# Four graph layers on one core: the weights' transfers issued by ScalarE instead of SyncE

## The chip, the cores and the metric

The kernel runs on one core of one Trainium2 chip. The time is the device time of one execution in microseconds, and several executions of the same kernel are compared by their median. A profile is one further execution, recorded instruction by instruction. The engines are named PE (TensorE), DVE (VectorE), ACT (ScalarE), POOL (GpSimd) and SP (SyncE, which here only issues transfers). Each engine takes its instructions in the order in which they were written down for it, and waits where an instruction needs another engine's result.

## The reference

64 graphs of 256 nodes with 512 features go through four layers. Each layer normalises, applies a ReLU, and adds what a graph layer makes of it to the residual `x`. Everything is float32.

```python
h = jnp.maximum(_layernorm(x), 0.0)
x = x + _L0_gnn_ref(h, adj, W_qk, W_v)                  # layer 0: masked score sums, softmax over nodes, times v
h = jnp.maximum(_layernorm(x), 0.0)
x = x + _L1_gnn_ref(h, adj, W, b, a_self, a_neigh)      # layer 1: graph attention, 8 heads of 64
h = jnp.maximum(_layernorm(x), 0.0)
x = x + _L2_gnn_ref(h, adj, Wp, bp, C)                  # layer 2: tanh(A * (Xc Xp^T)) Xp, 8 heads
h = jnp.maximum(_layernorm(x), 0.0)
x = x + _L3_gnn_ref(h, adj, nodemask, Wqk, Wv)          # layer 3: gated by q . (adj k), softmax over nodes, times v
```

## The kernel before

One graph at a time would leave every engine waiting, so the kernel overlaps about five graphs. The work of a graph is cut into some 120 named steps (`load`, `at`, `st0`, `hn0`, `sq0`, `sw0`, `ht0`, `qk0` and so on), and each step has a due time in a table. `TIMES` holds the steady state; graph `b` is due 60.2 us after graph `b-1`. The first six and the last five graphs have tables of their own (`FIRST`, `LAST`). A further table, `WEIGHTS`, gives due times to the steps that fetch and prepare the weights; these lie among the first graphs' steps. `Plan.sequence` sorts all steps of all graphs by due time, `Plan.run` writes them down in this order, and each engine's instructions are tied to that order. A due time is thus only a place in a queue; no clock is waited for.

The steps of a graph that matter here:

- `load` (L627): SP issues `x`, the adjacency rows `adj`, and the adjacency in 32x32 blocks `blocks`, four transfers by quarter.
- `st`, `rs`, `pw`, `sh`, `hn` (L652 to L681): layer norm and ReLU. DVE takes the statistics, POOL the power, DVE the shift, ACT writes `hn` (L680).
- `sq`, `sw`, `ht` (L685 to L696): the transposition of `hn`. DVE transposes 32x32 squares into `sq` (L613), SP sends `sq` to DRAM as `sq_d` (L700), and SP gathers `ht` from it in four transfers (L618). `ht` is what PE multiplies with the weights.
- `qk0`, `qk1`, `qe0`, `qe1` (L748 to L761): the query and key products of layer 0, and ACT's copies of them out of PSUM (L758). `score0` (L763) needs both copies; the value products `pv01` and `pv00` (L703, with `wv0_s`) stand behind it in PE's order.
- `fa0`, `fa1` (L789): the products of layer 1, with `w1_s`.
- `ea`, `ex` (L891, L914): ACT's Prelu and Exp of the attention.

The steps of the weights: `wqk`, `wv0`, `wv3` (L484, four transfers each), `w10` to `w13` and `w20` to `w23` (L490, four transfers each), `b1` and `b2` (L498), `c2` (L512, two), `wa` (L519, two), `mk` (L537), and `wn0` to `wn3` (L555, two each, one for each part of the product of layer 3's query and key weights). `mt`, `mv` and `mm` compute that product on PE and DVE, `sa` folds layer 1's attention vectors into its weights on DVE, and `ma` scales the product into `m3_s` on ACT.

Where a buffer is used several times, `take` and `done` (L400, L407) hand it from step to step through a first-in first-out list.

Of the kernel before, what the change touches and what calls it, by code (L numbers as in the profile page):

```python
# [16 lines left out]
P = 128  # L17
D = 512
KC = D // P
N = 256  # L20
NC = N // P
H = 8
# [365 lines left out]
class Graph:  # L388
# [5 lines left out]
    def step(self, name):  # L394
        def add(run):
            self.steps[name] = run
            return run
        return add
# [19 lines left out]
def tile_four_gnn_layers(ctx: ExitStack, tc: tile.TileContext, x, adj, nodemask,  # L418
# [5 lines left out]
    nc = tc.nc  # L424
# [14 lines left out]
    def keep(kind, count, shape, pool=None):  # L439

        plan.pools[kind] = [(pool or held).tile(shape, F32, name=f"{kind}{i}") for i in range(count)]
# [29 lines left out]
    c2_s = consts.tile([P, HP, P], F32)  # L471
# [5 lines left out]
    def weights():  # L477

        g = Graph(plan)
        step = g.step  # L480
        st = {}


        def plain(name, t, src):  # L484
            @step(name)
            def _():
                for r in range(4):
                    nc.sync.dma_start(t[r::4], src.rearrange("(k r d) e -> r d k e", k=KC, r=4)[r])

        def by_heads(name, k, t, src):  # L490
            @step(f"{name}{k}")
            def _():
                for r in range(4):
                    first = k * P + r * S
                    nc.sync.dma_start(t[r::4].rearrange("p (h u) -> p h u", h=H),
                                        src[:, first:first + S, :].rearrange("h d u -> d h u"))

        def to_all(name, t, src):  # L498
            @step(name)
            def _():  # L500
                nc.sync.dma_start(t, src.rearrange("h u -> (h u)").partition_broadcast(P))
        plain("wqk", wqk0_s, wqk0)
        plain("wv0", wv0_s, wv0)
        plain("wv3", wv3_s, wv3)
        for k in range(KC):
            by_heads("w1", k, w1_s[:, k, E:], w1)
            by_heads("w2", k, w2_s[:, k], w2)
        to_all("b1", b1_bc, b1)
        to_all("b2", b2_bc, b2)


        @step("c2")  # L512
        def _():
            for s in range(2):
                half = slice(s * U, (s + 1) * U)
                nc.sync.dma_start(c2_s[half, :, half], c2t.rearrange("(a s) k j -> s k a j", s=2)[s])


        @step("wa")  # L519
        def _():  # L520
            st["a"] = once.tile([P, 2, D], F32, name="a_bc", bufs=1)
            for s, a in enumerate((a_self, a_neigh)):
                nc.sync.dma_start(st["a"][:, s], a.rearrange("h u -> (h u)").partition_broadcast(P))

        def times_a(k):
            @step(f"sa{k}")
            def _():
                for s in range(2):
                    prod = once.tile([P, D], F32, name="prod", bufs=1)
                    nc.vector.tensor_mul(prod, w1_s[:, k, E:], st["a"][:, s])  # L530
                    nc.vector.tensor_reduce(w1_s[:, k, s * H:(s + 1) * H], prod.rearrange("p (h u) -> p h u", h=H),
                                            AX.X, OP.add)
        for k in range(KC):
            times_a(k)


        @step("mk")  # L537
        def _():
            st["mask"] = once.tile([B, N], F32, name="mask_rows", bufs=1)
            nc.sync.dma_start(st["mask"], nodemask)  # L540

        @step("mkp")
        def _():
            pm = g.take("bank", name="mask")
            for c in range(NC):
                nc.tensor.transpose(pm[:, c * B:(c + 1) * B], st["mask"][:, c * P:(c + 1) * P], ident[:B, :B])

        @step("mkv")
        def _():
            nc.vector.tensor_copy(mask_c, g["mask"][:, :NC * B].rearrange("p (c b) -> p c b", c=NC))  # L550
            g.done("mask")


        def part_of_m(e):
            @step(f"wn{e}")  # L555
            def _():
                st[f"wn{e}"] = w_n = once.tile([P, 2, KC, P], F32, name="w_n")
                for s in range(2):
                    first = s * D + e * P
                    nc.sync.dma_start(w_n[:, s], wqk3[:, first:first + P].rearrange("(k p) e -> p k e", p=P))  # L560

            @step(f"mt{e}")
            def _():
                for s in range(2):
                    pt = g.take("bank", name=f"wt{s}")
                    for k in range(KC):
                        nc.tensor.transpose(pt[:, k * P:(k + 1) * P], st[f"wn{e}"][:, s, k], ident)

            @step(f"mv{e}")
            def _():  # L570
                st["w_t"] = w_t = once.tile([P, 2, D], F32, name="w_t", bufs=1)
                nc.vector.tensor_copy(w_t[:, 0, :].rearrange("p (k d r) -> p k d r", k=KC, r=4),
                                      g["wt0"].rearrange("p (k r d) -> p k d r", k=KC, r=4))
                nc.vector.tensor_copy(w_t[:, 1, :], g["wt1"])
                g.done("wt0")
                g.done("wt1")

            @step(f"mm{e}")
            def _():
                for k in range(KC):  # L580
                    pm = g[f"m{k}"] if e else g.take("bank", name=f"m{k}")
                    nc.tensor.matmul(pm, st["w_t"][:, 0, k * P:(k + 1) * P], st["w_t"][:, 1, :],
                                     start=(e == 0), stop=(e == KC - 1))
        for e in range(KC):
            part_of_m(e)

        @step("ma")
        def _():
            for k in range(KC):
                nc.scalar.activation(m3_s[:, k, :], g[f"m{k}"], AF.Copy, scale=1.0 / math.sqrt(D))  # L590
                g.done(f"m{k}")


        @step("room")
        def _():
            setup.close()
            late = ctx.enter_context(tc.tile_pool(name="late", bufs=1, side="right"))
            keep("xp", 2, [P, NC, D], late)
            keep("xpt", 2, [P, HP, N], late)
            keep("xc", 1, [P, HP, N], late)  # L600
        return g
# [567 lines left out]
```

## Time and profile before

| | us |
|---|---|
| timed runs | 3900.15, 3894.99, 3899.66; median 3899.66 |
| profiled execution | 3905.45, of which 3903.3 from first to last instruction |
| PE busy | 3811.1 |
| DVE busy | 3033.7 |
| ACT busy | 1704.9 |
| POOL busy | 1264.8 |
| bytes moved | 717.62 MB, 184 GB/s in the mean |

A row of the groups reads: line, engine, operation, output and inputs, count, then the busy time in all and the mean of one in ns, then the engine's idle time just before these instructions and what ended most of it. The largest groups of PE are the products with the gathered `ht`:

```profile
L607 PE MATMUL bank<-w_s,ht 128*128 128x256 f32 (+2 forms) x3072 | 963.4, 464 | 30.6 <-DMA ht<-sq_d 24.5
L607 PE MATMUL bank<-wv_s,ht 128*128 128x512 f32 x2048 | 914.4, 594 | 0.1
```

A row of the time-ordered view reads: start, length, engine, line, operation, count, and in brackets the idle time before it and what ended it. A row with x4 is four neighbouring instructions run together. SPq marks SP's queue: the length is the time that SP spent on issuing, not the transfer. All transfers of the program are on one queue:

```profile
q1 hardware_dynamic: 1657328, 714.19, 74.7%
```

### The profile page before, as it was taken

What the parts mean: (1) busy time and instruction counts of PE and PEld (TensorE: products, weight loads), DVE (VectorE), ACT (ScalarE), POOL (GpSimd) and SP (SyncE); (2) the same over time, 40 slices, a digit from 0 to 9 for tenths busy, and PEclk for the clock granted to TensorE, in tenths of its full rate; (3) what the DMA queues carried; (4) which work ended last, traced back from release to release, by engine and by line L of the source; (5) the groups of instructions that cost most, each with busy time, mean ns of one, the idle gap of its engine ahead of it and who ended that gap; (6) DMA issues with size and microseconds to landing.
All of it is one profiled execution on the core that took longest, in us unless ns stands there. A gap on an engine that the chain in (4) does not pass through costs nothing.

```text
span 3903.3 us, 53632 instructions
## 1 busy us (share of the span) xinstructions
PE 3811.1 (98%) x17474; PEld 2375.3 (61%) x17474; DVE 3033.7 (78%) x7641; ACT 1704.9 (44%) x3333; POOL 1264.8 (32%) x1098
## 2 busy tenths in 40 slices
PE   7999999999999999999999999999999999999989
PEld 4756566566566666666666666666566665665564
DVE  6887778777877877877777788788788778777774
ACT  2444444444444444444444444444444444444342
POOL 1332323323323323323323333333233233233231
PEclk9999999999999999999999999999999999999989
DMA  8666777777777788777777877777778777777754
GB/s 211 174 189 172 179 194 174 196 193 179 194 189 184 194 185 189 192 185 181 190 186 186 196 182 187 191 181 191 191 176 200 187 181 192 187 179 193 172 145 107
DMA packets 1657607, 717.62 MB, mean 184 GB/s; under 512 B 1493936, under 2 KB 1549296, under 8 KB 1632752
## 3 DMA queue, kind: packets, MB, share of 16 engines
q1 hardware_dynamic: 1657328, 714.19, 74.7%
q8 instruction: 140, 2.29, 0.3%
q14 instruction: 139, 1.14, 0.1%
HBM read 477.56 MB, written 236.45 MB: 183 GB/s over the span
## 4 chain that ended last, share of the span: by engine, by line
PE 74%; DVE 7%; DMA 4%; SPq 2%; issue 1%; POOL 1%; ACT 1%; DVEq 0%; POOLq 0%; ACTq 0%
PE bank L607 44%; PE bank L928 10%; PE bank L1016 6%; PE bank L1030 5%; PE bank L1102 5%; PE bank L994 3%; DVE junk L852 2%; DVE sq L613 1%; DMA hn<-sq_d 1%; SPq L618 1%; DMA ht<-sq_d 1%; DVE shift L673 1%; PE bank L768 1%; PE bank L718 1%; DVE stats L657 1%
## 5 line engine op out<-in xcount | busy, mean ns | idle before, releaser
L607 PE MATMUL bank<-w_s,ht 128*128 128x256 f32 (+2 forms) x3072 | 963.4, 464 | 30.6 <-DMA ht<-sq_d 24.5
L607 PE MATMUL bank<-wv_s,ht 128*128 128x512 f32 x2048 | 914.4, 594 | 0.1
L607 PEld LDWEIGHTS bank<-w_s,ht 128*128 128x128 f32 x3072 | 572.9, 192 | 364.4 <-issue 215.6
L607 PEld LDWEIGHTS bank<-wv_s,ht 128*128 128x128 f32 x2048 | 380.8, 191 | 426.2 <-issue 410.8
L904 POOL TENSOR_TENSOR pair<-pair,negt 128x1024 f32<-128x1024 f32 x256 | 600.5, 2367 | 50.6 <-ACT pair L897 46.4
L680 ACT ACTIVATE hn<-xt,shift,rstd 128x512 f32<-128x512 f32 x512 | 388.7, 806 | 448.6 <-DVE shift L673 430.3
L928 PEld LDWEIGHTS bank<-feats,pair 128*128 128x128 f32 x4096 | 485.0, 194 | 47.9 <-issue 25.5
L897 ACT ACTIVATE pair<-all,ec 128x256 f32<-128x256 f32 x1024 | 417.2, 494 | 200.1 <-DMA all<-er_d 196.3
L928 PE MATMUL bank<-feats,pair 128*128 128x65 f32 x4096 | 480.8, 276 | 10.2 <-ACT pair L916 10.2
L1055 ACT ACTIVATE pair<-pair 128x512 f32<-128x512 f32 x512 | 294.8, 623 | 420.6 <-DVE pair L1048 420.2
L852 DVE CUSTOM_DVE_ANT_0 junk<-all,adj 128x256 f32<-128x256 f32 x1024 | 444.0, 434 | 35.2 <-DMA all<-er_d 2.1
L607 PE MATMUL bank<-m_s,ht 128*128 128x512 f32 x1024 | 465.9, 599 | 1.3 <-DVE pair L1048 0.8
L668 POOL TENSOR_TENSOR rstd<-rstd,power 128x2 f32<-128x2 f32 x256 | 180.6, 706 | 813.4 <-DVE rstd L664 804.9
L1048 DVE TENSOR_TENSOR pair<-bank,at 128x512 f32<-128x512 f32 x512 | 327.4, 683 | 107.7 <-PE bank L1016 107.0
L1083 POOL TENSOR_TENSOR xt<-xt,hn 128x512 f32<-128x512 f32 x64 | 111.5, 1742 | 924.6 <-DMA hn<-sq_d 657.9
L613 DVE STREAM_TRANSPOSE sq<-hn 128x512 f32<-128x512 f32 x512 | 337.7, 690 | 58.9 <-ACT hn L680 58.9
L657 DVE BATCH_NORM_STATS2 stats<-xt 128x6 f32<-128x512 f32 x512 | 327.2, 680 | 36.4 <-POOL xt L1083 28.6
L910 DVE TENSOR_TENSOR pair<-pair,all 128x1024 f32<-128x1024 f32 x256 | 325.9, 1292 | 9.9 <-DMA all<-m_d 7.5
L607 PEld LDWEIGHTS bank<-m_s,ht 128*128 128x128 f32 x1024 | 189.2, 190 | 213.5 <-issue 207.1
L953 POOL TENSOR_TENSOR xt<-xt,o 128x256 f32<-128x256 f32 x256 | 181.2, 729 | 386.6 <-DVE rs L941 225.1
L916 ACT ACTIVATE pair<-pair 128x1024 f32<-128x1024 f32 x256 | 262.2, 1047 | 45.1 <-DVE pair L910 39.6
L1016 PE MATMUL bank<-xc,xpt 64*128 64x256 f32 x2048 | 255.8, 389 | 1.8 <-ACT xc L1002 1.0
(77 smaller groups left out, 3866.9 us busy)
## 6 DMA issues: line engine op xcount, KB each, us to landing
sq_d<-sq SPq DMA_DIRECT2D x384, 512.0 KB
ht<-sq_d SPq DMA_DIRECT2D x1024, 128.0 KB
all<-er_d SPq DMA_DIRECT2D x128, 1024.0 KB
all<-m_d SPq DMA_DIRECT2D x64, 1024.0 KB
xt<-in_x_dram SPq DMA_DIRECT2D x64, 512.0 KB
xpt<-sq_d SPq DMA_DIRECT2D x256, 128.0 KB
hn<-sq_d SPq DMA_DIRECT2D x256, 128.0 KB
out_dram<-xt SPq DMA_DIRECT2D x64, 512.0 KB
```

Source lines behind the costliest of these rows:

```text
L607: nc.tensor.matmul(p, ht[:, k, c * P:(c + 1) * P], w[:, k], start=(k == 0), stop=(k == KC - 1))
L613: nc.vector.transpose(sq.rearrange("p (r k c i) -> p c k r i", r=4, k=KC, c=NC)[:, c], t[:, c])
L657: nc.vector.bn_stats(stats[:, c, :], g["xt"][:, c, :])
L680: nc.scalar.activation(hn[:, c, :], g["xt"][:, c, :], AF.Relu, bias=st["shift"][:, c:c + 1], scale=st["rstd"][:, c:c + 1])
L852: nc.vector.tensor_tensor_reduce(junk, g["en"][:, h, :], g["adj"][:, c, :], 1.0, -BIG, OP.add, OP.max, st["mx"][:, c, h:h + 1])
L897: nc.scalar.activation(e[:, s, j, :], g["es"][:, h, :], AF.Prelu, bias=st["ec"][:, j, H + h:H + h + 1], alpha=0.2)
L904: nc.gpsimd.tensor_tensor(e, e, g["negt"][:, None].to_broadcast([P, 2, NC, N]), OP.add)
L910: nc.vector.tensor_tensor(e, e, g["m"][:, 2 * p:2 * p + 2, None, :].to_broadcast([P, 2, NC, N]), OP.subtract)
L928: nc.tensor.matmul(po[:, h % 4, :], e[:, s, j, i * P:(i + 1) * P], feats[:, j, h, :], start=(j == 0), stop=(j == NC - 1))
L1016: nc.tensor.matmul(ps[s][:, m, :], g["xpt"][half, p, m * P:(m + 1) * P], g["xc"][half, p, :], start=True, stop=True)
L1048: nc.vector.tensor_tensor(th[:, s], g[f"ps{p}{s}"].rearrange("p (m n) -> p m n", m=NC), g["at"], OP.mult)
L1055: nc.scalar.activation(g[f"th{p}"][:, s], g[f"th{p}"][:, s], AF.Tanh)
```

## The change

The 59 transfers that the weights' steps issue go out from ACT's queue. The steps stay where they were in the plan. The PSUM banks that `mt` takes also get the part's number in their name; the names are a key in a dictionary.

```diff
         def plain(name, t, src):
                 for r in range(4):
-                    nc.sync.dma_start(t[r::4], src.rearrange("(k r d) e -> r d k e", k=KC, r=4)[r])
+                    nc.scalar.dma_start(t[r::4], src.rearrange("(k r d) e -> r d k e", k=KC, r=4)[r])
...
         def by_heads(name, k, t, src):
-                    nc.sync.dma_start(t[r::4].rearrange("p (h u) -> p h u", h=H),
+                    nc.scalar.dma_start(t[r::4].rearrange("p (h u) -> p h u", h=H),
...
         def to_all(name, t, src):
-                nc.sync.dma_start(t, src.rearrange("h u -> (h u)").partition_broadcast(P))
+                nc.scalar.dma_start(t, src.rearrange("h u -> (h u)").partition_broadcast(P))
...
-                nc.sync.dma_start(c2_s[half, :, half], c2t.rearrange("(a s) k j -> s k a j", s=2)[s])
+                nc.scalar.dma_start(c2_s[half, :, half], c2t.rearrange("(a s) k j -> s k a j", s=2)[s])
...
-                nc.sync.dma_start(st["a"][:, s], a.rearrange("h u -> (h u)").partition_broadcast(P))
+                nc.scalar.dma_start(st["a"][:, s], a.rearrange("h u -> (h u)").partition_broadcast(P))
...
-            nc.sync.dma_start(st["mask"], nodemask)
+            nc.scalar.dma_start(st["mask"], nodemask)
...
-                    nc.sync.dma_start(w_n[:, s], wqk3[:, first:first + P].rearrange("(k p) e -> p k e", p=P))
+                    nc.scalar.dma_start(w_n[:, s], wqk3[:, first:first + P].rearrange("(k p) e -> p k e", p=P))
...
-                    pt = g.take("bank", name=f"wt{s}")
+                    pt = g.take("bank", name=f"wt{s}{e}")
...
-                g.done("wt0")
-                g.done("wt1")
+                g.done(f"wt0{e}")
+                g.done(f"wt1{e}")
```

More of the change, by code (lines that the diff above doesn't have):

```diff
@@ L572, in _ @@
                 nc.vector.tensor_copy(w_t[:, 0, :].rearrange("p (k d r) -> p k d r", k=KC, r=4),
-                                      g["wt0"].rearrange("p (k r d) -> p k d r", k=KC, r=4))
-                nc.vector.tensor_copy(w_t[:, 1, :], g["wt1"])
-                g.done("wt0")
-                g.done("wt1")
+                                      g[f"wt0{e}"].rearrange("p (k r d) -> p k d r", k=KC, r=4))
+                nc.vector.tensor_copy(w_t[:, 1, :], g[f"wt1{e}"])
+                g.done(f"wt0{e}")
+                g.done(f"wt1{e}")
             @step(f"mm{e}")
```

## The prediction

> **What bounds the kernel now.** I read the page's first two parts, then stage windows, then the time-ordered view of the first 130 us. The page:
>
> ```profile
> span 3903.3 us, 53632 instructions
> PE 3811.1 (98%) x17474; PEld 2375.3 (61%) x17474; DVE 3033.7 (78%) x7641; ACT 1704.9 (44%) x3333; POOL 1264.8 (32%) x1098
> ```
>
> TensorE (PE) is busy 3811.1 of 3903.3 us, so 92.2 us of PE idleness is all that a better order can win. Where it lies, from the stage windows (start:end, length, busy time and count per engine, PE clock, DMA share, GB/s):
>
> ```profile
> 0.00:100.00 100.00, 72.05 (x269) 43.69 (x270) 65.72 (x162) 25.36 (x52) 18.37 (x26) 0.97 0.82 210
> 100.00:200.00 100.00, 95.40 (x478) 70.85 (x478) 81.28 (x208) 44.08 (x85) 37.08 (x32) 0.91 0.71 174
> 1000.00:2000.00 1000.00, 993.98 (x4616) 622.36 (x4615) 793.81 (x2016) 450.99 (x883) 331.38 (x288) 1.00 0.77 188
> ```
>
> 28.0 us of it is in the first 100 us, 4.6 in the second; in the steady part only 0.6%. The weights' transfers all lie before 146 us. So the change can only shift the start, and PE, nearly full after 500 us, carries a shift to the end. The start (start us, length, engine, line, operation; the bracket gives the idle time before it and its releaser; SPq is SyncE's queue):
>
> ```profile
> 12.96 0.55 SPq L700 DMA_DIRECT2D sq_d<-sq  x1
> 20.11 2.65 SPq L488 DMA_DIRECT2D wv_s<-in_L_gnn_W_v_dram  x4
> 22.81 2.57 SPq L495 DMA_DIRECT2D w_s<-in_L_gnn_W_dram  x4
> 24.23 0.27 ACT L758 COPY qk<-bank 128x128 f32<-128x128 f32 x1 [5.95 <-PE bank L607]
> 25.12 0.27 ACT L758 COPY qk<-bank 128x128 f32<-128x128 f32 x1 [0.63 <-PE bank L607]
> 25.44 0.88 PE L768 MATMUL bank<-qk,at 128*128 128x64 f32 x6 [0.18 <-ACT qk L758]
> 26.44 3.67 PE L607 MATMUL bank<-wv_s,ht 128*128 128x512 f32 x8
> 34.71 2.02 PE L607 MATMUL bank<-wqk_s,ht 128*128 128x128 f32 x16 [0.94 <-DMA ht<-sq_d]
> 38.26 1.52 ACT L680 ACTIVATE hn<-xt,shift,rstd 128x512 f32<-128x512 f32 x2 [1.16 <-DVE shift L673]
> 42.48 0.38 SPq L700 DMA_DIRECT2D sq_d<-sq  x1
> 53.06 5.47 PE L607 MATMUL bank<-w_s,ht 128*128 128x272 f32 x16 [2.68 <-DMA ht<-sq_d]
> ```
>
> The weights go out from SP in time: the first Wv matmul at 26.44 waits for nothing. The two query copies of graph 0 stand 0.9 us apart on ScalarE (ACT), and PE needs the second at once.
>
> **What the Trainium skill says.** DMA: Bandwidth & Descriptors, section Issuing engines are not separate DMA queues: transfers of all issuing engines share the same DMA engines, and a second issuer saves only sequencer time; the page of before shows one busy hardware queue, so no run here bears on it yet. Perfetto Trace Analysis, section DMA Instruction — HWDGE: a recorded issue begins once its semaphores are satisfied and ends when the sequencer is free for its next instruction. The trace agrees as far as it goes: SP's issues follow each other without overlap, 602 to 968 ns each for w2. TensorE: Matmul & The Clock Gate, section What's actually happening: the PE clock halves after idling. The trace agrees: after 2.68 us of idling the w1 matmuls at 53.06 take 5.47/16 = 342 ns, the same form at 125.99 takes 5.61/24 = 234 ns.
>
> **The change, part by part.** 59 weight transfers leave SP's queue; their issue times in the time-ordered view add up to 42.4 us, 0.72 us each (8 w_n 5.55, 4 wqk 2.65, 2 a 1.40, 4 wv0 2.65, 16 w1 11.63, 2 b 1.03, 16 w2 11.43, mask 0.79, 2 c2 1.28, 4 wv3 3.94). They enter ACT's in-order queue at the same steps. ACT's other work, and all of PE, DVE and POOL, keep their order. The renamed PSUM banks (wt0 to wt00 and so on) cost nothing: the order of takes and returns, and PE's order in the built program, are unchanged. No trace has a DMA issue on ACT; I price it between SP's undisturbed 0.60 and its mean 0.72 us, taking 0.65.
>
> A second thing follows from the built program's waits. All transfers rotate over eight completion semaphores, and each issue first waits until the last user of its semaphore has landed. In the new program both queues share the eight, so an ACT issue can wait for an SP transfer, with ACT's arithmetic behind it.
>
> (1) *Graph 0 to its first ht: a gain.* sq was ready at 9.73 (the DVE transposes start at 8.31 and take 1.42) but sq_d left at 12.96, after graph 1's loads, which stood behind w_n and wqk (1.17 + 2.65 us of issue). That hold of 3.2 us goes. Against it, xt now competes with w_n from the start: 512 KB at this stretch's 210 GB/s is 2.5 us, so the delay is 0 to 2.5; I take 0.9. Net -2.3 (bounds -3.2 to -0.7).
>
> (2) *The second query copy: the large loss.* Between the two copies stand wv0 x4 and w1 x4. Without waiting: 22.2 (first copy's end, 24.5 - 2.3) + 8 x 0.65 = 27.4, against 25.12 before. With the shared semaphores the fourth wv0 waits for the last quarter of graph 1's ht: ht0's issues end at 20.07 - 2.3 = 17.8; sq_d takes 3.4 (25.48 to 28.90), four ht issues 3.3, landing 2.5 (32.17 to 34.71): 27.0. Then five issues, 3.2: 30.2. So the score and value matmuls behind the copy, and all of PE, come +2.3 to +6 later; I take +5.2, the gain of (1) already inside. The gain of graph 1's sq_d (ready at 19.03, issued at 25.48) is worthless, since PE reaches graph 1 only after this.
>
> (3) *PE clock.* PE idles about 6 us before those matmuls instead of 0.2. At the price of the 53.06 row, 16 x 108 ns = 1.7; bounds 0 to 1.7, taken 1.
>
> (4) *hn of graph 0, layer 1.* w_n x2 and w1 x4 now stand between graph 1's second query copy (ended 37.10) and hn (38.26): 6 x 0.65 = 3.9 up to the 5.5 they took on SP, less the 1.1 that ACT waited for the shift: +2.8 to +4.4. Returned: sq was complete at 40.82 while sq_d left SP at 42.48, 1.7. Net +1.1 to +2.7, taken +2, all onto PE, which was idle 2.68 us for this ht at 53.06.
>
> (5) *The rest, nearly nothing.* The fourth w1 group, w2's first three, mask, c2 and w_n fall into ACT's idle stretches (6.05 us before 51.70, 6.74 before 59.18, 7.19 before 72.78, 5.63 before 85.54, 6.93 before 94.82). wv3, at some 143 us, is hidden by 10.2 us of ACT idleness before 156.2. Only w2's last four meet a busy ACT (96.25 to 103.7): 2.6 us before the Prelu of the next graph, of which I put 0 to 2 on PE, taken 0.8.
>
> (6) *Given back.* From 100 to 500 us PE idles 18.4 us; part of it shrinks when PE is late and the others are not. 0 to 4, taken -1.
>
> Sum: 5.2 + 1 + 2 + 0.8 - 1 = **+8.0 us**, on the profiled span 3911.3. Bounds: 2.3 + 0 + 1.1 + 0 - 4 = -0.6, and 6 + 1.7 + 2.7 + 2 = +12.4. The profiled execution, 3905.45, is 5.8 above the timed median of 3899.66 (3894.99 to 3900.15); the shift added to that median gives **3908**.
>
> **Rivals.** *SP's relief wins.* ACT's issues are short and the semaphore waits are satisfied when reached. Then (1)'s -2.3 to -3.2 stays, and (2) falls away if the second copy starts before 25.1. For it: SP held sq_d three times, by 3.2, 6.4 and 1.7 us, and ACT is 25% busy in the first 100 us. Against: even without a wait, eight issues at 0.60 put the copy at 27.0. A lucky clock could help: the PE clock is 0.5 from 101 to about 117 us at full work, some 7 us that another phase may not lose. Time: 3899.7 - 3, less 0 to 7 for the clock: 3890 to 3897, about 3893.
>
> *Hidden.* Loss (2) is its no-wait size and the rest sits in the 33 us of PE idleness of the first 200: +2 to +6, about 3903. For it: small terms; against: step (4)'s ht is already what PE waits for.
>
> *Semaphores chain further.* The waits between queues pass from group to group, for example an ACT issue held by ht, holding hn, holding the next sq_d and ht. Each turn costs the 3.4 to 3.5 us of an sq_d landing; two more turns than I counted give +15, 3915.
>
> That the change does nothing is excluded: the built program has the issues on ACT.
>
> **How the numbers follow.** A measurement of this kernel can tell about 0.2%, 7.8 us, from no change. The forecast, its size around +8: 0.45, of it 0.27 above the bound and 0.18 within. Hidden: 0.22, within. Chained: 0.23, above. Relief: 0.10, below. So slower 0.27 + 0.23 = 0.50, within 0.18 + 0.22 = 0.40, faster 0.10. The range takes the forecast's bounds, half of relief below and the nearer part of chained above: 3895 to 3917; the forecast alone has 3899 to 3912.
>
> **What would show it.** After: DMA issues on ACT from 0.7 us; the first sq_d near 10.6; the second query copy of graph 0 at 27 to 31; the first Wv matmul at 28 to 32, with an idle time from ACT; hn at 45 to 47 instead of 38.26; the w1 matmuls at 60 to 62 instead of 53.06; steady windows unchanged. If the first Wv matmul comes before 27, or the w1 matmuls before 55, I am wrong in the start; if these are late and the end is not, step (6) is too small.

## The result

The changed kernel takes 3924.98 us in the median of four runs (3919.33 to 3930.32), the kernel before 3897.71 beside it (3894.99 to 3900.15). The ratio is 1.007, with a 95% interval of 1.0053 to 1.0087: +27 us, between 21 and 34. A later comparison of the same two kernels gave 1.0062 (1.0046 to 1.0077), +24 us. The forecast was +8. The direction was right, the size a third of what came.

The page of the changed kernel, its first two parts:

```profile
span 3917.5 us, 53618 instructions
PE 3811.3 (97%) x17474; PEld 2375.6 (61%) x17474; DVE 3037.3 (78%) x7641; ACT 1704.8 (44%) x3333; POOL 1262.0 (32%) x1098
```

PE has the work it had (3811.3 against 3811.1 us), and ACT too. The 14.2 us by which the span grew are idleness of PE. They are fewer than the 27 us of the medians because this profile is of the shortest of the four runs (3919.33), while that of the kernel before (3905.45) is of an execution longer than its four timed ones. The stage windows (start:end, length, busy time and count per engine, PE clock, DMA share, GB/s) say where:

```profile
0.00:100.00 100.00, 62.54 (x216) 36.51 (x216) 52.77 (x130) 19.56 (x43) 14.74 (x24) 0.90 0.77 176
100.00:200.00 100.00, 88.58 (x439) 66.16 (x440) 86.42 (x216) 43.85 (x84) 33.56 (x29) 0.91 0.69 184
1000.00:2000.00 1000.00, 994.33 (x4611) 621.31 (x4611) 792.80 (x2016) 449.24 (x882) 333.34 (x288) 1.00 0.78 187
```

PE idles 37.5 us in the first 100 (28.0 before) and 11.4 in the second (4.6 before). The steady part is as it was. The time-ordered view of the changed kernel, the rows that answer those shown of before (ACTq is ACT's queue, with the time spent on issuing and on waits between the issues of one row):

```profile
14.78 1.41 SPq L700 DMA_DIRECT2D sq_d<-sq  x1
24.78 2.05 PE L607 MATMUL bank<-wqk_s,ht 128*128 128x128 f32 x16 [0.78 <-DMA ht<-sq_d]
25.97 0.27 ACT L758 COPY qk<-bank 128x128 f32<-128x128 f32 x1 [5.19 <-PE bank L607]
25.98 7.63 ACTq L488 DMA_DIRECT2D wv_s<-in_L_gnn_W_v_dram  x4
33.65 5.43 ACTq L495 DMA_DIRECT2D w_s<-in_L_gnn_W_dram  x4
39.12 0.27 ACT L758 COPY qk<-bank 128x128 f32<-128x128 f32 x1 [12.88 <-DMA w_s<-in_L_gnn_W_dram]
39.43 1.54 PE L768 MATMUL bank<-qk,at 128*128 128x64 f32 x6 [12.44 <-ACT qk L758]
40.77 6.41 PE L607 MATMUL bank<-wv_s,ht 128*128 128x512 f32 x8
57.04 0.81 ACT L680 ACTIVATE hn<-xt,shift,rstd 128x512 f32<-128x512 f32 x1 [4.07 <-DMA w_s<-in_L_gnn_W_dram]
59.33 0.34 SPq L700 DMA_DIRECT2D sq_d<-sq  x1
69.32 5.59 PE L607 MATMUL bank<-w_s,ht 128*128 128x272 f32 x16 [2.16 <-DMA w_s<-in_L_gnn_Wp_dram]
```

Three things are to be seen. The first query products start at 24.78 instead of 23.04, although SP was to be relieved. The two query copies stand 13.1 us apart, with eight DMA issues between them, and PE waits 12.44 us for the second. The first Wv products last 6.41 us instead of 3.67. Together the first w1 products (69.32 against 53.06) are 16.3 us late. A further loss comes after this row; it is on VectorE, where the forecast had not looked. The time-ordered view of the changed kernel, VectorE, GpSimd and PE from 85 us:

```profile
85.65 0.41 DVE L852 CUSTOM_DVE_ANT_0 junk<-all,adj 128x256 f32<-128x256 f32 x1
92.97 9.26 POOL L904 TENSOR_TENSOR pair<-pair,negt 128x1024 f32<-128x1024 f32 x4 [12.04 <-ACT pair L897]
93.26 2.08 DVE L736 TENSOR_SCALAR w<-w,tot 128x2 f32<-128x2 f32 x1
95.45 2.21 DVE L865 TENSOR_SCALAR low<-mx 128x16 f32<-128x16 f32 x1
97.70 2.27 DVE L866 SCALAR_TENSOR_TENSOR low<-mx,low 128x16 f32<-128x16 f32 x1
100.00 2.26 DVE L867 TENSOR_TENSOR mx<-mx,low 128x16 f32<-128x16 f32 x1
102.98 0.38 PE L873 MATMUL bank<-ident,mx 128*8 128x128 f32 x2 [3.32 <-DVE xt L742]
```

Four operations on a few elements last over 2 us each, as long as one of GpSimd's four operations L904 beside them, and PE waits 3.32 us for what follows. The same stretch of the kernel before, from a second profile of it (b_again below):

```profile
68.32 0.42 DVE L852 CUSTOM_DVE_ANT_0 junk<-all,adj 128x256 f32<-128x256 f32 x1 [0.67 <-DMA all<-er_d]
76.48 0.17 DVE L866 SCALAR_TENSOR_TENSOR low<-mx,low 128x16 f32<-128x16 f32 x1
76.69 0.17 DVE L867 TENSOR_TENSOR mx<-mx,low 128x16 f32<-128x16 f32 x1
77.02 9.27 POOL L904 TENSOR_TENSOR pair<-pair,negt 128x1024 f32<-128x1024 f32 x4 [15.27 <-ACT pair L897]
```

Here the same operations take 0.17 us, and VectorE is done at 76.86, 0.16 us before GpSimd begins. Between the first w1 products and PE's first products with `pair` (L928) the changed kernel needs 50.0 us (69.32 to 119.35), the kernel before 45.2 in its first profile and 44.6 in its second. So 16.3 us are lost at the start and 4.8 more here: 21.1 at L928 against the first profile, 22.9 against the second, which lies within the interval of the time.

### The profile page after: what moved, and what is told of

It reads as the page before. It is cut to its first block, busy times and chain, and to the rows that moved or that the text cites. A ratio compares the mean times of both kernels' runs of the same rounds, so it can differ in the third digit from the quotient of the medians.

```text
span 3917.5 us, 53618 instructions
## 1 busy us (share of the span) xinstructions
PE 3811.3 (97%) x17474; PEld 2375.6 (61%) x17474; DVE 3037.3 (78%) x7641; ACT 1704.8 (44%) x3333; POOL 1262.0 (32%) x1098
## 4 chain that ended last, share of the span: by engine, by line
PE 73%; DVE 7%; DMA 4%; SPq 2%; issue 1%; POOL 1%; ACT 1%; DVEq 0%; POOLq 0%; ACTq 0%
PE bank L607 43%; PE bank L928 10%; PE bank L1016 6%; PE bank L1030 5%; PE bank L1102 5%; PE bank L994 3%; DVE junk L852 3%; DVE sq L613 2%; DMA hn<-sq_d 1%; SPq L618 1%; DVE shift L673 1%; DMA ht<-sq_d 1%; PE bank L768 1%; PE bank L718 1%; SPq L1076 1%
## 5 line engine op out<-in xcount | busy, mean ns | idle before, releaser
L607 PE MATMUL bank<-w_s,ht 128*128 128x256 f32 (+2 forms) x3072 | 960.9, 463 | 30.2 <-DMA ht<-sq_d 21.4
L904 POOL TENSOR_TENSOR pair<-pair,negt 128x1024 f32<-128x1024 f32 x256 | 600.4, 2366 | 53.0 <-ACT pair L897 44.8
L928 PEld LDWEIGHTS bank<-feats,pair 128*128 128x128 f32 x4096 | 485.5, 195 | 47.3 <-issue 28.1
L928 PE MATMUL bank<-feats,pair 128*128 128x65 f32 x4096 | 481.2, 276 | 9.9 <-ACT pair L916 9.9
L852 DVE CUSTOM_DVE_ANT_0 junk<-all,adj 128x256 f32<-128x256 f32 x1024 | 440.0, 430 | 34.4 <-DMA all<-er_d 1.1
```

Of the source, the lines that this page charges most:

```text
L607: nc.tensor.matmul(p, ht[:, k, c * P:(c + 1) * P], w[:, k], start=(k == 0), stop=(k == KC - 1))
L852: nc.vector.tensor_tensor_reduce(junk, g["en"][:, h, :], g["adj"][:, c, :], 1.0, -BIG, OP.add, OP.max, st["mx"][:, c, h:h + 1])
L904: nc.gpsimd.tensor_tensor(e, e, g["negt"][:, None].to_broadcast([P, 2, NC, N]), OP.add)
L928: nc.tensor.matmul(po[:, h % 4, :], e[:, s, j, i * P:(i + 1) * P], feats[:, j, h, :], start=(j == 0), stop=(j == NC - 1))
```

## Experiments

Times are ratios to the kernel before on the same chip; 0.001 is 3.9 us. "First Wv" is the start of the first Wv products on PE, "first w1" that of the first w1 products.

### The start

**e0_after_again** is the changed kernel, once more.

> The changed kernel once more, beside the others on one chip: 1.005 to 1.009 of before, if the 27 us between the medians are more than the 18 us by which PE is late at 140 us of the profile.

1.0062 (1.0046 to 1.0077). First Wv 39.15, first w1 65.86. The loss is stable, its parts vary by a few us between executions (PE idles 11.15 us here and 12.44 there).

**e1_only_wv0_w1**: the kernel before, with only the twelve transfers `wv0`, `w11` and `w10` on ACT.

```diff
-                    nc.sync.dma_start(t[r::4], src.rearrange("(k r d) e -> r d k e", k=KC, r=4)[r])
+                    (nc.scalar if name == "wv0" else nc.sync).dma_start(t[r::4], src.rearrange("(k r d) e -> r d k e", k=KC, r=4)[r])
...
-                    nc.sync.dma_start(t[r::4].rearrange("p (h u) -> p h u", h=H),
+                    (nc.scalar if f"{name}{k}" in ("w10", "w11") else nc.sync).dma_start(t[r::4].rearrange("p (h u) -> p h u", h=H),
```

> Kernel before, with only the 12 transfers of wv0, w11 and w10 on ACT, the other 47 on SP as before. Theory A (the hold of the second query copy of graph 0 behind these issues is the loss): the two copies are 8 to 13 us apart instead of 0.9, the first Wv matmul comes at 34 to 40 instead of 26.4, and the time is 1.003 to 1.007 of before, most of what the whole change costs. Theory B (the loss is spread over many groups of transfers, each with its own wait): the copies may be apart, but the time is within 1.002 of before.

1.0034 (1.0022 to 1.0046), +13 us. The first query products come at 22.86, the copies at 24.06 and 38.82, first Wv at 40.47. These twelve transfers make about half of the loss by themselves.

**e2_all_but_wv0_w1**: the reverse, the changed kernel with these twelve back on SP.

```diff
-                    nc.scalar.dma_start(t[r::4], src.rearrange("(k r d) e -> r d k e", k=KC, r=4)[r])
+                    (nc.sync if name == "wv0" else nc.scalar).dma_start(t[r::4], src.rearrange("(k r d) e -> r d k e", k=KC, r=4)[r])
...
-                    nc.scalar.dma_start(t[r::4].rearrange("p (h u) -> p h u", h=H),
+                    (nc.sync if f"{name}{k}" in ("w10", "w11") else nc.scalar).dma_start(t[r::4].rearrange("p (h u) -> p h u", h=H),
```

> Changed kernel, with wv0, w11 and w10 back on SP, the other 47 transfers on ACT. Theory A: the copies are 0.9 us apart again and the time is within 0.9985 to 1.002 of before. Theory B: the time keeps at least half of the loss, 1.0035 or more.

1.0022 (1.0013 to 1.0031), +9 us, between the two theories. The copies are 0.9 us apart, and still a third of the loss is there: +13 and +9 add up to nearly the whole. The query products start at 25.61. So the narrow account, in which everything is the second query copy, is not enough.

**e5_hold_long** and **e7_hold_short** put nothing but a hold into the kernel before: 28 and 12 idle ACT operations between the two copies of graph 0. Their results are not used.

```diff
+                if b == 0 and c == 1:
+                    hold = work.tile([P, N], F32, name="hold", tag="scratch", bufs=1)
+                    for _ in range(28):
+                        nc.scalar.activation(hold, wqk0_s[:, 0:2].rearrange("p k e -> p (k e)"), AF.Relu)
```

> Kernel before, all transfers on SP, with 28 idle activations (their result is not used) on ACT between the two query copies of graph 0, some 11 to 15 us: the hold alone, without any transfer on ACT. Theory A: PE is late by 11 to 15 us behind it, the groups of 130 us stay late by about as much, and the time is 1.003 to 1.006 of before. If a late start is made good later (theory D), the time is within 1.002.

> Kernel before with 12 idle activations on ACT between the two query copies of graph 0, 5 to 6.5 us: the size of eight issues at 0.65 us without any wait. Theory A: PE is 5 to 6 us late behind it, and the time is 1.001 to 1.002 of before, clearly less than with the long hold. So much the issues alone would cost; the rest of the change's loss is then waiting for landings.

With 28, PE idles 11.85 us ahead of the score products and the time is 1.0023 (1.0014 to 1.0032), +9 us, less than expected; with 12 it idles 4.69 us and the time is 1.001 (1.0004 to 1.0017), +4 us. A hold at this place costs about 0.8 us for each us, and keeps costing it to the end: 9.0/11.85 and 3.9/4.69 (the intervals of both include 1). By this estimate the changed kernel's 12.44 us are worth some 10 us.

**e3_copies_first**: the changed kernel with `wv0` and `w11` planned behind the second copy.

```diff
-    "wn0": 292.900, "mt0": 293.000, "wqk": 293.100, "mv0": 294.200, "wa": 294.700, "mm0": 295.100, "wv0": 295.500,
-    "w11": 295.600, "w10": 296.200, "sa1": 296.700, "sa0": 297.000, "wn1": 298.500, "w13": 298.600, "mt1": 299.000,
+    "wn0": 292.900, "mt0": 293.000, "wqk": 293.100, "mv0": 294.200, "wa": 294.700, "mm0": 295.100, "wv0": 295.910,
+    "w11": 295.920, "w10": 296.200, "sa1": 296.700, "sa0": 297.000, "wn1": 298.500, "w13": 298.600, "mt1": 299.000,
```

> Changed kernel, with the due times of wv0 and w11 put just behind the second query copy of graph 0, so that ACT makes both copies first and issues then. Theory A in the narrow sense (the copy is what matters): copies 0.9 us apart, time near before, 1.000 to 1.002. Rival C (the late arrival of Wv is what matters, and the copy was only the first to show it): PE waits for wv0 itself, issued from about 27 us and landed at some 37, so the first Wv matmul comes at 34 to 40 and the time is still 1.003 to 1.007.

1.0056 (1.0044 to 1.0068): nothing gained beyond the spread. The copies are adjacent (26.66 and 27.56), but the time-ordered view has now the wait one step on:

```profile
40.05 5.35 PE L607 MATMUL bank<-wv_s,ht 128*128 128x512 f32 x8 [11.29 <-DMA w_s<-in_L_gnn_W_dram]
```

The weights themselves come too late. (The bracket names `w_s`, since transfers share semaphores; the semaphores that these products wait for are those of the four `wv0`, of which the last was issued at 35.55.) In ACT's order a transfer goes out only after ACT's earlier arithmetic, and this arithmetic waits for PE's query products. On SP nothing of that kind stood ahead of them: `wv0` left at 20.11, before the query products had begun. Ahead of the copy they hold it, behind it they are late; both cost 11 to 12 us of PE.

**e6_wv0_early**: they are planned ahead of ACT's waits instead (`wv0` at 293.750, `w11` at 294.750, otherwise the changed kernel).

> Changed kernel, with wv0 due right behind graph 0's hn and w11 behind the attention vectors, that is issued on ACT from some 9 us, before graph 1's hn. Theory A: no issue stands between the query copies, which are 0.9 us apart; PE is at most 4 us late from the earlier traffic and graph 1's hn held behind w11; time 0.999 to 1.003. If the shared semaphores by themselves cost as much (theory E), graph 1's hn, its sq_d and ht move by 8 us or more and the time stays at 1.004 or more.

1.0037 (1.0024 to 1.005). First Wv moves from 40.77 to 32.07, and the time falls by about 10 us, to just above theory A's range. But now PE waits 3.16 us for the query products, which start at 26.62: the early weights go out beside the first graphs' loads.

**e4_pool_queue**: all 59 go out from GpSimd's queue, with eight semaphores of their own (in each of the change's lines `nc.gpsimd.dma_start`).

> All 59 weight transfers on GpSimd's queue at the same places. In the built program its transfers rotate over eight completion semaphores of their own, so SP's never wait for them nor they for SP's, and ACT holds no transfer. Theory A (in-order hold plus shared semaphores): copies of graph 0 are 0.9 us apart, SP's first sq_d leaves by 12, and the time is 0.998 to 1.002 of before. Rival (any second queue costs, since its packets share the transfer engines with x and ht): ht lands later than before and the time is 1.003 or more.

1.0059 (1.0047 to 1.0071), although ACT issues nothing and shares no semaphore. `sq_d` leaves at 12.83, as before; the row of PE in the time-ordered view shows the price:

```profile
30.17 3.75 PE L607 MATMUL bank<-wqk_s,ht 128*128 128x128 f32 x16 [5.79 <-DMA ht<-sq_d]
```

`ht` is issued until 21.67 and PE starts 8.5 us later; in the kernel before it is 3.0 (20.07 to 23.04). On the single queue of before, `ht` stood ahead of `wv0` and `w1`; from a second queue they run beside it. The Trainium skill, DMA: Bandwidth & Descriptors, section Queues, rings and completion order, says that each DMA engine takes packets from the queues in turn; the two numbers agree. A second queue thus takes away the priority that SP's order gave. GpSimd's queue is of another kind than ACT's (the pages list it as software_dynamic, ACT's as hardware_dynamic), so the size does not carry over. Nor is this row the whole price: the first w1 products are 9 to 10 us later than in the two profiles of the kernel before, L928 18 to 20 us, and between the two three of VectorE's operations last over 2.4 us, the kind of loss that is taken apart below under the later transfers.

### SyncE's relief

**b_again** is the kernel before itself, profiled once more.

> The kernel before itself, profiled once more. Theory U (its recorded profile was an unlucky one: PE ran at half clock from 101 to about 117 us): another profile has no such stretch there, the first group of the second graphs' 272-wide products (x24, at 125.99 in the first profile) starts at 117 to 121, and the span is 3893 to 3899. Then the change's shift at this mark is about 23 to 27 us, which agrees with the timed difference. Rival V (the half clock belongs to this point of the program): the mark stands at 124 to 127 again and the span at 3902 to 3905; then 6 to 10 us of the timed loss arise later than 200 us. The time itself: ratio 1.000.

0.9998 (0.9989 to 1.0006). Neither account holds as written: the mark stands at 124.38 and the PE clock from 100 to 150 us is 0.86 (0.83 in the first profile), so the half clock belongs to this place; yet the span is 3897.4, 5.9 less, because PE idles less from 200 to 3000 us. The 272-wide mark moves with the clock, by 6 us between kernels whose time is the same (120.2 to 126.0), so I leave it and read L928, which comes ahead of that stretch.

**e8_first_group**: the kernel before with only the first eight transfers (`wn0`, `wqk`, `wa`) on ACT.

> Only the first eight transfers (w_n x2, wqk x4, a x2) are issued by ScalarE; everything else as before. Theory S (these eight are what turned the forecast gain of step (1) into a loss, by waits on shared semaphores and by sharing the transfer engines with the first graph's loads): the first query products start at 24.2 to 25.6 instead of 23.04, the two query copies stay 0.9 us apart, the time is 3 to 1 us longer, ratio 1.0002 to 1.0008. Rival (the forecast's step (1), SyncE relieved): the first query products at 20.0 to 22.3, the time 1 to 3 us shorter, ratio 0.9992 to 0.9998.

1.0007 (0.9999 to 1.0015), first query products at 26.76. The start is even later than I had put it, and nothing of a gain is to be seen. In the changed kernel's trace, two of SP's issues of graph 0's `blocks` wait for w_n, issued by ACT on the same semaphores (4.2 us in all, so that the four take until 8.52 instead of 4.72; 4.7 us in this run's trace), so graph 1's loads leave no earlier than before (8.57 against 8.68), and `sq_d` behind them later.

**e11_load_behind_sq** tests the premise: the kernel before, all transfers on SP, with graph 1's loads and statistics planned behind graph 0's `sq_d`.

```diff
-        "load": 233.000, "st0": 233.700, "rs0": 233.900, "pw0": 234.100, "at": 234.300, "sh0": 234.700,
+        "load": 234.450, "st0": 234.460, "rs0": 234.470, "pw0": 234.480, "at": 234.490, "sh0": 234.700,
```

> The kernel before with the second graph's loads moved in SyncE's queue from ahead of the first graph's write of the transposed rows to behind it (its statistics move with it on VectorE); no transfer changes its queue. Theory R (SyncE's own hold of 3.1 us ahead of this write is real and its removal reaches PE): the write leaves at 9.8 to 10.3 instead of 12.96, the first query products start at 20.5 to 21.8 instead of 23.04, the time is 1 to 2.5 us shorter, ratio 0.9994 to 0.9998; this is what step (1) promised, had without a second queue. Rival (the gather behind the write meets the second graph's loads on the transfer engines and PE finds its next wait instead): products at 22.5 to 24, ratio 0.9998 to 1.0005.

1.0004 (0.9998 to 1.0011): the rival. `sq_d` leaves at 9.51 instead of 12.96, and PE gains 0.4 us. Two rows of the time-ordered view:

```profile
9.51 0.36 SPq L700 DMA_DIRECT2D sq_d<-sq  x1
22.65 3.78 PE L607 MATMUL bank<-wqk_s,ht 128*128 128x128 f32 x16 [4.84 <-DMA ht<-sq_d]
```

`ht` is issued at 15.94, no more than 0.5 us earlier than in the kernel before (16.45): `sq_d` now runs beside graph 1's loads, which follow it at once. The 3.2 us for which SP held `sq_d` were not worth 3.2 us, even without a second queue.

### The later transfers

**e9_late_only**: the later 39 alone on ACT; `wn0`, `wqk`, `wa`, `wv0`, `w10` and `w11` are SP's. **e9_again** is the same kernel.

```diff
-                    nc.scalar.dma_start(t[r::4], src.rearrange("(k r d) e -> r d k e", k=KC, r=4)[r])
+                    (nc.sync if name in ("wqk", "wv0") else nc.scalar).dma_start(t[r::4], src.rearrange("(k r d) e -> r d k e", k=KC, r=4)[r])
...
-                    nc.scalar.dma_start(t[r::4].rearrange("p (h u) -> p h u", h=H),
+                    (nc.sync if f"{name}{k}" in ("w10", "w11") else nc.scalar).dma_start(t[r::4].rearrange("p (h u) -> p h u", h=H),
...
-                nc.scalar.dma_start(st["a"][:, s], a.rearrange("h u -> (h u)").partition_broadcast(P))
+                nc.sync.dma_start(st["a"][:, s], a.rearrange("h u -> (h u)").partition_broadcast(P))
...
-                    nc.scalar.dma_start(w_n[:, s], wqk3[:, first:first + P].rearrange("(k p) e -> p k e", p=P))
+                    (nc.sync if e == 0 else nc.scalar).dma_start(w_n[:, s], wqk3[:, first:first + P].rearrange("(k p) e -> p k e", p=P))
```

> Only the later 39 transfers (all but w_n0, wqk, a, wv0 and the first two quarters of w1) are issued by ScalarE. Theory T (ScalarE's transfers slow the first graphs' loads and gathers wherever they run beside them, and so the later ones cost too): the start up to the first w1 products (53.06) is as before within 1.5 us, the 272-wide mark is 4 to 9 us later than in a profile of before without the half clock, the time is 3 to 6 us longer, ratio 1.0008 to 1.0016. Rival (the forecast's step (5), nearly nothing): mark within 2 us, time +0 to +1.5, ratio 1.0000 to 1.0004.

> The later 39 transfers alone on ScalarE, once more. If the first result holds: 8 to 14 us longer than before, ratio 1.002 to 1.0036, the 272-wide mark at 129 to 133, and the second w_n issue near 77 again held by about 4 us between two groups of Prelus. If the first was an accident of its few runs: ratio 1.0008 to 1.0016.

1.0028 (1.0018 to 1.0039) and 1.0017 (1.0007 to 1.0026): +11 and +7 us, where step (5) had 0.8 and theory T 3 to 6. The first w1 products are where they were (53.15 and 53.50).

ACT's w_n issue, held by about 4 us between two groups of Prelus in both profiles (72.83 to 77.23, 72.84 to 76.99), was the first suspect. **e12_late_wn3_back** takes only this away (`e in (0, 3)` in the last line of the diff), **e13_hold_prelu** puts only this into the kernel before: 12 idle ACT operations, as in e7_hold_short, ahead of the last group of Prelus.

> As the later 39 alone on ScalarE, but the last two w_n transfers (issued at 72.83 and 77.23) are SyncE's again, so that no transfer stands between the groups of Prelus; 37 are left on ScalarE. Theory H (the hold of the Prelus by a wait of the w_n issue is what the later transfers cost): the last group of Prelus starts at 73 to 75 instead of 77.65, the copy of mr at 84 to 86 instead of 87.45, the mark at 125 to 128 instead of 130.70, the time 2 to 6 us above before, ratio 1.0005 to 1.0016. Rival B (transfers of two queues beside each other slow SyncE's gathers everywhere): mark 129 to 132, ratio 1.002 to 1.003.

> The kernel before with 12 idle ScalarE operations (their results are not used) ahead of the last group of Prelus of the first graph, 4.5 to 5 us; no transfer is moved. Theory H: the copy of mr at 86.5 to 89 instead of 84.10, the 272-wide mark 2.5 to 5 us later than 124.4 to 126, the time 2 to 5 us longer, ratio 1.0005 to 1.0013. Rival B (such a hold is hidden, since ScalarE was idle 5.64 us ahead of mr): mark within 1 us, ratio 0.9996 to 1.0004.

1.0022 (1.0013 to 1.0031) without the hold, 1.0002 (0.9994 to 1.001) with the hold alone. The hold is hidden; that theory fell. The trace of e12 shows VectorE's stretched operations again. The profiles, in the order of GpSimd's distance behind VectorE:

| kernel | GpSimd's first L904 minus VectorE's first L852, us | VectorE operations of 2.0 to 2.6 us | first w1 to L928, us |
|---|---|---|---|
| b_again | 8.70 | 0 | 44.6 |
| e5_hold_long | 8.63 | 0 | 44.5 |
| e13_hold_prelu | 8.52 | 0 | 43.8 |
| e11_load_behind_sq | 8.47 | 0 | 43.8 |
| e7_hold_short | 8.43 | 0 | 43.9 |
| e1_only_wv0_w1 | 8.28 | 1 | 44.1 |
| e8_first_group | 8.11 | 2 | 44.8 |
| before | 8.04 | 2 | 45.2 |
| e6_wv0_early | 7.53 | 4 | 48.8 |
| changed kernel | 7.32 | 4 | 50.0 |
| e3_copies_first | 7.23 | 4 | 48.7 |
| e0_after_again | 7.07 | 4 | 50.0 |
| e12_late_wn3_back | 6.98 | 4 | 48.7 |
| e9_late_only | 6.72 | 4 | 50.7 |
| e9_again | 5.67 | 4 | 51.3 |
| e2_all_but_wv0_w1 | 4.20 | 4 | 52.4 |

VectorE needs 8.54 us for this chain (68.32 to 76.86 in b_again). With a lead of about 8.5 us it is done before GpSimd begins; with less, one operation waits for each of GpSimd's, up to all four. Two late ones cost nothing that can be seen, four cost 4 to 8 us. The Trainium skill, SBUF — State Buffer, section Who interferes with whom, says that a VectorE instruction with two inputs in SBUF contends with a GpSimd instruction that reads SBUF, that some with one input can contend too, in modes that use both ports, and that in these modes the engine that issues second is blocked for the other's whole instruction. The durations agree: 2.0 to 2.6 us beside L904's 2.34 to 2.56. Every kernel of the table with the later transfers on ACT has four late operations, the others have two at most (e4_pool_queue is left out, since GpSimd issues transfers there).

**e14_dve_late** makes VectorE late in the kernel before, with no transfer moved: five idle additions ahead of graph 0's first maxima.

```diff
                 c = i // 2
+                if b == 0 and i == 1:
+                    hold = work.tile([P, N], F32, name="hold", tag="scratch", bufs=1)
+                    for _ in range(5):
+                        nc.vector.tensor_tensor(hold, wqk0_s[:, 0:2].rearrange("p k e -> p (k e)"),
+                                                wqk0_s[:, 2:4].rearrange("p k e -> p (k e)"), OP.add)
```

> The kernel before with five idle VectorE additions (0.42 us each, results not used) ahead of the first graph's first row maxima, 2.1 us; no transfer is moved. Theory R (the race with GpSimd's L904): three or four of VectorE's last small operations of these maxima last over 2 us, PE's first products with pair (L928) start 47.5 to 51 us after the first w1 products (43.8 to 45.2 in the kernel before and wherever the race was won), the time is 4 to 9 us longer, ratio 1.0010 to 1.0023. Rival D (a plain delay): none is stretched beyond those of before, 44 to 47 us, time +0 to +2, ratio 1.0000 to 1.0005.

1.0023 (1.0016 to 1.0031), +9 us for 2.25 us of additions. The time-ordered view:

```profile
68.50 2.25 DVE L853 TENSOR_TENSOR hold<-wqk_s 128x256 f32<-128x256 f32 x5
76.73 9.83 POOL L909 TENSOR_TENSOR pair<-pair,negt 128x1024 f32<-128x1024 f32 x4 [12.96 <-ACT pair L902]
76.96 2.44 DVE L857 CUSTOM_DVE_ANT_0 junk<-all,adj 128x256 f32<-128x256 f32 x1
84.56 2.03 DVE L736 TENSOR_SCALAR w<-w,tot 128x2 f32<-128x2 f32 x1
88.01 0.59 PE L878 MATMUL bank<-ident,mx 128*8 128x128 f32 x2 [6.11 <-DVE xt L742]
```

Four operations are stretched, three of them still among the maxima themselves (lines stand five lower here), and L928 comes 51.6 us after the first w1 products, just past what was expected. The later transfers' loss is reproduced without a transfer.

**e15_late_pool_held** and **e16_after_pool_held** are the reverse: GpSimd is held ahead of its first L904, in the kernel with the later 39 on ACT and in the changed kernel. Only the first of the added operations needs the Prelu's result; none is used.

```diff
                 e = g[f"e{p}"]
+                if b == 0 and p == 1:
+                    hold = small.tile([P, 8], F32, name="hold", bufs=1)
+                    nc.gpsimd.tensor_tensor(hold[:, :NC], e[:, 0, 0, :NC], power, OP.add)
+                    for _ in range(60):
+                        nc.gpsimd.memset(hold, 0.0)
                 nc.gpsimd.tensor_tensor(e, e, g["negt"][:, None].to_broadcast([P, 2, NC, N]), OP.add)
```

> As the later 39 alone on ScalarE, with one small addition and 60 small memsets on GpSimd (results not used), some 2 to 5 us, between the first graph's first Prelus and GpSimd's first L904. Theory R: VectorE is done before GpSimd begins, none of L735 to L867 lasts over 0.5 us, the first products with pair start 44.5 to 47.5 us after the first w1 products instead of 50.7 and 51.3, the time is 1 to 5 us above before, ratio 1.0003 to 1.0013 instead of 1.0028 and 1.0017. Rival D: the products stay 49 to 52 us behind, ratio 1.0017 to 1.0028.

> The changed kernel with the same GpSimd hold. Theory R: none of L735 to L867 is stretched, the first products with pair start 44.5 to 47.5 us after the first w1 products instead of 50.0, the time is 4 to 8 us below the changed kernel's, ratio to before 1.0042 to 1.0056 instead of 1.0062 and 1.007. Rival D: unchanged, 1.0058 to 1.0072.

e15 has 1.0006 (0.9998 to 1.0015) instead of 1.0028 and 1.0017. Its time-ordered view:

```profile
76.46 9.64 POOL L908 MEMSET hold<- 128x8 f32 x60
80.74 0.23 DVE L736 TENSOR_SCALAR w<-w,tot 128x2 f32<-128x2 f32 x1
81.53 0.17 DVE L867 TENSOR_TENSOR mx<-mx,low 128x16 f32<-128x16 f32 x1
100.67 10.16 PE L933 MATMUL bank<-feats,pair 128*128 128x65 f32 x48 [4.05 <-ACT pair L921]
```

The memsets took 9.64 us, not 2 to 5, so GpSimd itself became late and PE waited 4.05 us for `pair`; even so L928 follows 46.3 us after the first w1 products instead of 50.7 and 51.3. e16 has 1.0055 (1.0042 to 1.0068), L928 46.9 us after instead of 50.0. Its shift of 3 to 6 us against the changed kernel has the expected sign, but the intervals overlap.

None of these kernels is faster than the kernel before.

## Why the prediction was wrong in its size

**Step (1), graph 0's first `ht`: the sign failed.** Forecast -2.3, with every bound a gain; measured +1.74 (24.78 against 23.04), in e8_first_group alone +3.7. Two premises fell. SP was not relieved at this place, since its `blocks` issues waited for ACT's w_n on a shared semaphore; I had followed these waits only from SP to ACT, not back. And the 3.2 us hold of `sq_d` was not what set `ht` (e11_load_behind_sq). xt's competition with w_n, for which 0.9 was set, cost hn 0.2 (7.64 against 7.46).

**Step (2), the second query copy: right mechanism and place, too small.** The price of an issue on ACT was right (wv0: 606 to 772 ns, median 622; 0.65 was taken), and eight took 5.3 us. (SP's shortest issue of w2 in the trace of before is 598 ns, not 602; nothing hangs on it.) The waits were 7.8 us instead of 2.8. I had counted one, the fourth wv0 behind graph 1's `ht`. The trace has three: 2.8 us ahead of the third wv0 for the landing of the first, 2.2 us for that `ht`, and 2.9 us ahead of the second w1 for graph 2's `adj`. With step (1)'s 4.0 the copy came at 39.12 instead of 30.2, and first Wv at +14.3 instead of +5.2.

**Step (3), the PE clock.** The score products took 1.54 us instead of 0.88 and the first Wv group 6.41 instead of 3.67: 3.4 us against 1 (bound 1.7). The granted clock fell to 0.50 during the idle time and stayed there to about 46 us, so the slow phase went on through most of the Wv group, which the bound, priced from 16 matmuls of another form, left out. In the second profile of the changed kernel the same two groups lost 1.8 us: the end of the slow phase is not fixed by the idle time.

**Step (4), hn of graph 0, was right in its mechanism.** Graph 1's second query copy was 15.9 us late and hn 18.8: a hold of 2.9, in the forecast's 2.8 to 4.4. `sq_d` was 16.9 late: 1.9 returned, forecast 1.7. The net of 1.0 lies just below the lower bound (1.1); 2 was taken.

**Step (5), the rest: it failed, and no bound covered it.** ACT did have the idle stretches. But the question was asked of ACT alone, not of whether VectorE would still be done before GpSimd begins. Counted from the first w1 products, GpSimd's first L904 starts after 23.0 to 23.9 us in the eight profiles with the later 39 on ACT and no hold, and after 24.2 to 25.4 us in the nine with them on SP. VectorE's first L852 starts after 16.3 to 18.9 us in the former and 15.7 to 17.4 us in the latter (e14_dve_late apart). In the changed kernel's profile VectorE is not late at all (16.3 us, against 17.4 and 16.5 in the two profiles of the kernel before). There it is GpSimd that is early, because ACT's Prelus, whose results it needs, get their input `all` 8.2 us after its last issue instead of 10.2. The rows of the changed kernel, then those of b_again:

```profile
79.14 0.42 SPq L840 DMA_DIRECT2D all<-er_d  x1
87.29 1.70 ACT L897 ACTIVATE pair<-all,ec 128x256 f32<-128x256 f32 x4 [5.32 <-DMA all<-er_d]
61.11 0.43 SPq L840 DMA_DIRECT2D all<-er_d  x1
71.33 1.71 ACT L897 ACTIVATE pair<-all,ec 128x256 f32<-128x256 f32 x4 [8.34 <-DMA all<-er_d]
```

So in this profile it was a transfer made faster, not one made slower, that cost VectorE its lead. In e2_all_but_wv0_w1 and e9_again VectorE is later as well (18.9 and 17.4 us). A shift of 1 to 2 us between the two engines became 7 to 11 us, 4.8 of it visible in the changed kernel's trace by L928. Why `all` lands sooner stays open; that SP's queue no longer carries the weights around it would fit. How much of the slower gathers is sharing of the DMA engines and how much shared semaphores was not separated either.

**Step (6)**: nothing was visibly given back; the lag of 21 to 23 us at L928 is the time's +24 to +27 within its interval. The other kernels agree: behind b_again at L928 are e7_hold_short and e8_first_group by 3.5 and 3.6 us (time +4 and +3), the two profiles of the later 39 by 7.5 and 8.4 (+11 and +7), e5, e6, e2 and e1 by 11.0 to 12.9 (+9 to +14), e16, e4, e3 and the changed kernel by 18.2 to 22.9 (+21 to +27). A single execution can still differ by several us later on: the profile of e9_late_only is of the shortest of its eight runs (3898.99).

Of the rivals, relief is out: the issue time that SP saved did not show as a gain. "Hidden", which ended at +6, is out too. "Semaphores chain further" had the right kind of mechanism and the right direction, but at +15 it allowed for two extra turns at the start and nothing behind. The range ended at +17 because every term in it had been bounded by issue times and a single wait, not by what a late issue does to the next engine.

By parts, the single experiments give +13 (the twelve), +3 (the first eight, not resolved from none) and +7 to +11 (the later 39): +23 to +27, the whole of the loss within the intervals.

## What to carry over

A transfer on an engine that also computes leaves only when that engine's earlier arithmetic has been released, and whatever it waits for holds the arithmetic behind it; count both, and follow shared semaphores in both directions. A second queue takes from the first the priority that its order gave, so transfers that are off the critical path can delay those that are on it. And before a shift of 2 us is called hidden, look for pairs of engines that exclude each other, as VectorE and GpSimd do here: when one chain ends just before the other engine starts, delaying the one or hastening the other can cost four times as much (2.25 us cost 9 in e14_dve_late).

## What the runs showed of the hardware that was not expected

- A VectorE operation on 128x2 or 128x16 elements, 0.17 to 0.23 us by itself, lasts 2.0 to 2.3 us beside GpSimd's additions of 128x1024, one for each of GpSimd's operations; in the kernel before VectorE's chain ends within 0.2 to 0.5 us of GpSimd's start, and its two profiles fall on different sides (0 and 2 operations late).
- Sixty GpSimd memsets of 128x8 took 9.64 us, 0.16 each; VectorE's small operations beside them were not slowed (0.17 to 0.23 us).
- Where PE idles 4.7 to 14 us ahead of them, the granted clock is 0.50 at their start and the first eight Wv matmuls take 4.8 to 6.4 us instead of 3.60 to 3.67. The loss does not follow the idle time: 4.69 us idle gave 5.29 us (e7_hold_short), 14.05 gave 5.35 (e1_only_wv0_w1), 12.44 gave 6.41 (the changed kernel).
